# GNN layer on one core: GpSimd gathers every row, transfers carry two node blocks, store rounds lose their empty steps

## The chip, the cores and the metric

One core of a Trainium2 chip runs one program. The time is device microseconds from launch to end, as the runs measure it; a profiled execution gives the trace. The core has TensorE (PE, matmuls; its weight loads are PEld), VectorE (DVE), ScalarE (ACT), GpSimd (POOL) and SyncE (SP). POOL and SP issue most of the transfers here, each in its own fixed order. Sixteen DMA engines move the data.

## The reference

One message-passing layer with a residual and a normalization: 50,000 nodes of 160 features, 1,650,000 edges sorted by destination, four attributes an edge. The last 50,000 edges in the list before sorting are loops from each node to itself.

```python
ss, vv = (s[src], v[src])            # s, v: 64 scalars and 32 vectors of a node
e0 = sh[:, 0:1]; e1 = sh[:, 1:4]     # edge attributes
dot = jnp.einsum('eui,ei->eu', vv, e1)
out0 = C0 * (ss * e0 @ W1 + dot * INV3 @ W2)
...
m = jnp.concatenate([out0, out1.reshape(-1, 3 * MUL1)], axis=1)
m_agg = jax.ops.segment_sum(m, dst, num_segments=n)
...
return x + jax.nn.relu(h)            # h: m_agg times Ws and Wv
...
x = _layernorm(x + _L0_gnn_ref(...))
```

The message is linear in the source row for each attribute. So the kernel may first sum the source rows over a node's edges, weighted by each of the four attributes, and apply the weights after that.

## The kernel before

**Units and pairs.** A unit is 128 edges. Its source rows are gathered into one slot of a tile `xg`, 128 partitions by 160 numbers (`gather`, L314), by one indirect DMA on POOL (L319), whose offsets are a column of `si`. Six units make a group, and two groups a pair: 12 units, one `xg` tile; the pool `rows` holds four such tiles. There are 1,044 pairs; the loop over them (L800) writes out the program, and its order of lines is roughly that of the work.

**What a pair does.** DVE builds a one-hot matrix of the destinations within a window of 32 (`hot`, L328), then multiplies it by the four attributes (`ha`, L331), one pair ahead of its use. PE multiplies `ha` by the gathered rows, unit after unit, and adds up in `ps` (`group_sums`, L343). DVE turns the result into `sums` (L349). Every second pair fills a chunk of four groups; PE applies the combined weights (`phc`, L579) and ACT copies the result out (`hp`, L581). The engines other than SP run in an order that a scheduler makes when the program is built; SP's is as written (L799).

**Node blocks.** Rows of the output come in 391 blocks of 128 nodes. For a block, `ahead` (L588) loads its rows of x and its nodes' own attributes `sa`, seven pairs before the chunks that it needs are complete; `own` (L609) does the loop edge's part (`yx`, L623, then L627 and L629) three pairs before; `block` (L633) adds the chunks with another one-hot matmul (`phb`, L639); then come the normalization (`norm1` to `norm3`, the last being L197 and L199) and `do_send` (L733), which stores the block, eight pairs after the chunk's end. All of these transfers stand on SP's queue.

**Packs.** The loop edges have to be taken out of the list. Except for the first 100 groups, edges go through sixteen packs (`pack`, L408), each up to 128 rows of 790 edges: a pack reads its rows, marks and counts the loop edges, moves the other edges together by copies under a mask in steps of 1, 2, 4, 8 and 16 (L504 to L511, first for the own attributes `pra`, then for the edges `prow`), and stores each row with its own attributes into DRAM (`edges`, `selves`) at a place that SP reads from a table (`store`, L539; `put`, L561). Seventeen store rounds of up to 16 stores each make up a pack. `load` (L247) then reads the packed edges in segments of 20 groups, ten pairs, and `place` (L278) turns them into `si`, destinations and attributes.

**How a pack's steps are dealt.** A pack is a list of steps, some of them empty (`None`). The loop deals the list evenly over the pairs from the pack before to this pack's due time (L834 to L842).

**The helper.** `HELP` (L70) names engines that fetch rows beside POOL. SP has a period of 72 units: for one unit in 72 it reads 128 offsets, 32 at a time, from `ro` (`fetch`, L665; `ro` is made by ACT at L274) and issues 128 plain DMAs of one row each into `xr` (L676), over four pairs. `gather` then leaves that unit out, and `group_sums` uses `xr` as the last rows of its pair.

Behind the loop stands a general path (from L858) that runs only if one of the checks made on the way found data outside the bounds; the run's data are within them.

Of the kernel before, what the change touches and what calls it, by code (L numbers as in the profile page):

```python
# [38 lines left out]
F32 = mybir.dt.float32  # L39
# [6 lines left out]
ET = mybir.EngineType  # L46
# [3 lines left out]
P = 128  # L50
MUL0, MUL1 = 64, 32
D = MUL0 + 3 * MUL1
NK = 4
# [13 lines left out]
PG = 2  # L67
SG = 20

HELP = {ET.SP: 72}  # L70
HEAD = 100
RP = 128
RS = 16
KM = 31
# [29 lines left out]
def tile_gnn_resnorm(ctx: ExitStack, tc: tile.TileContext, x, src, dst, attr, W1, W2, W3, W4, W5, Ws, Wv, out, n_edges):  # L104
    nc = tc.nc
    N = x.shape[0]
    NBLK, NB, GA, G, NU, NG, L, NH, NR, FAR = plan(N, n_edges)
# [83 lines left out]
    def norm2(pool, mv, n):  # L191
        rstd = pool.tile([P, 1], F32, name="rstd")
        nc.scalar.activation(rstd[:n], mv[:n, 1:2], AF.Sqrt, bias=eps_t[:n])  # L193
        return rstd

    def norm3(pool, y, mv, rstd, n):
        nc.vector.reciprocal(rstd[:n], rstd[:n])  # L197
        o = pool.tile([P, D], F32, name="o")
        nc.vector.tensor_scalar(o[:n], y[:n], mv[:n, 0:1], rstd[:n], op0=ALU.subtract, op1=ALU.mult)  # L199
        return o  # L200

# [14 lines left out]
    nblocks = math.ceil(N / P)  # L216
# [8 lines left out]
    with tc.tile_pool(name="once", bufs=1) as once, tc.tile_pool(name="raw", bufs=2) as rawp, \  # L225
# [1 line left out]
            tc.tile_pool(name="far", bufs=3) as farp, \  # L227
            tc.tile_pool(name="ops", bufs=3) as op, tc.tile_pool(name="sums", bufs=4) as sump, \
            tc.tile_pool(name="hp", bufs=alive + 4) as hpp, tc.tile_pool(name="node", bufs=3) as np_, \
            tc.tile_pool(name="ahead", bufs=7) as aheadp, \  # L230
            tc.tile_pool(name="psC", bufs=1, space=PSUM) as psC, tc.tile_pool(name="psK", bufs=2, space=PSUM) as psK, \
            tc.tile_pool(name="psP", bufs=1, space=PSUM) as psP, tc.tile_pool(name="psA", bufs=2, space=PSUM) as psA, \
            tc.tile_pool(name="psM", bufs=2, space=PSUM) as psM, ExitStack() as later_pools:
# [8 lines left out]
        dq = nc.sync  # L242
# [22 lines left out]
        def cast(loaded):  # L265
            s, n, ri, sf, df, af = loaded
            if ri is not None:
                rf = rawp.tile([P, 2, P], F32, name="rf")
                begun.append(nc.scalar.copy(rf[:n], ri[:n]))
                sf, df = rf[:n, 0, :], rf[:n, 1, :]  # L270
            if HELP:

# [85 lines left out]
        def row_start(r):  # L358

            lo, hi = (math.floor(r * L * (1 - 1 / degree)) - 2 * FAR - 2, math.ceil(r * L * (1 - 1 / degree)) + 2 * FAR + 2)  # L360
            return (max(lo, 0), hi if r else 0), (max(math.floor((EH + r * L) / degree) - FAR - 2, 0),
                                                  math.ceil((EH + r * L) / degree) + FAR + 2)

        edges = dram.tile([1, (row_start(NR - 1)[0][1] + L) * C], F32, name="edges")
        selves = dram.tile([1, (row_start(NR - 1)[1][1] + W) * NK], F32, name="selves")
        edge_bytes = edges.bitcast(U8).rearrange("o f -> (o f)")
        self_bytes = selves.bitcast(U8).rearrange("o f -> (o f)")
        rows_stored = [0]
# [39 lines left out]
        def pack(c):  # L408

            r0 = c * RP  # L410
            n = min(RP, NR - r0)
            e0 = EH + r0 * L
            e = slice(e0, e0 + n * L)
            steps, T = [], {}
# [154 lines left out]


            for head, j in [(False, j) for j in range(RS)] + [(True, 0)]:
                steps += [partial(store, head, j), None, None, None]
            return steps + [stored]

        def apply_weights(at, ng):
# [8 lines left out]
        def rows_of(b):  # L584
            nb = min(P, N - b * P)
            return nb, slice(b * P, b * P + nb)

        def ahead(b):  # L588

            nb, row = rows_of(b)  # L590
            xt = aheadp.tile([P, D], F32, name="xt")
            dq.dma_start(xt[:nb], x[row, :])

            assert rows_stored[0] == NR or row_start(rows_stored[0])[1][0] >= row.stop
            sa = aheadp.tile([P, NK], F32, name="sa")
            dq.dma_start(sa[:nb], selves[0, row.start * NK:row.stop * NK].rearrange("(n k) -> n k", k=NK))
            return xt, sa

        def nodes(b):

# [32 lines left out]
        def block(b, xt, t, hot2):  # L633
# [3 lines left out]
            for i, c in enumerate(cs):  # L637
# [7 lines left out]
        pairs = [(s, g, min(PG, NG - g, (s + 1) * SG - g)) for s in range(NSC)  # L645
                 for g in range(s * SG, min(NG, (s + 1) * SG), PG)]
        batches, helped = {}, {}
        for h, (eng, period) in enumerate(HELP.items()):
            first = PG * G + h * period // 2
            nbatch = P // ROWS[eng]  # L650
            while True:
                at = [int(first + i * period / nbatch) // (PG * G) for i in range(nbatch)]
                q = at[-1] + 2
                if q >= len(pairs) or pairs[q][2] < PG:
                    break
                s, g, ng = pairs[q]
                u = (g - s * SG + ng) * G - 1 - len(helped.get(q, []))
                helped.setdefault(q, []).insert(0, (eng, h))
                for i, p in enumerate(at):
                    batches.setdefault(p, []).append((eng, h, q, s, u, i))  # L660
                first += period
# [49 lines left out]
        hps, of_nodes, resid, rstds, outs = {}, {}, {}, {}, {}  # L711
# [4 lines left out]
                of_nodes[b] += (nodes(b),)  # L716

        def do_ahead(b):
            of_nodes[b] = ahead(b)

        def do_own(b):
            of_nodes[b] = own(b, *of_nodes.pop(b))
# [5 lines left out]
            rstds[b] = norm2(np_, resid[b][1], rows_of(b)[0])  # L728

        def do_store(b):  # L730
            outs[b] = norm3(np_, *resid.pop(b), rstds.pop(b), rows_of(b)[0])

        def do_send(b):  # L733
            nb, row = rows_of(b)
            dq.dma_start(out[row, :], outs.pop(b)[:nb])

        def do_cast(s):
            raws[s] = cast(raws[s])
# [179 lines left out]
    with tc.tile_pool(name="edges2", bufs=2) as ep, tc.tile_pool(name="ops2", bufs=2) as op, \  # L918
            tc.tile_pool(name="node2", bufs=1) as np_, tc.tile_pool(name="psA2", bufs=2, space=PSUM) as psA, \
            tc.tile_pool(name="psF2", bufs=1, space=PSUM) as psF:  # L920
        with tc.For_i(0, blocks, 1) as b:
            u0 = table(0, b)
            u1 = table(1, b)
            acc = np_.tile([NBLK, NK, D], F32, name="acc")
            nc.vector.memset(acc, 0.0)

            with tc.For_i(u0, u1, GA) as u:
                u = nc.s_assert_within(u, 0, NU - GA, skip_runtime_bounds_check_because="below u1")
                s_t = ep.tile([P, GA], I32, name="s_t")
                d_t = ep.tile([P, GA], I32, name="d_t")  # L930
                a_t = ep.tile([P, GA, NK], F32, name="a_t")
                e = ds(u * P, GA * P)
                nc.sync.dma_start(s_t, src1[e].rearrange("(p j) o -> p (j o)", j=GA))
                nc.sync.dma_start(d_t, dst1[e].rearrange("(p j) o -> p (j o)", j=GA))
                nc.sync.dma_start(a_t, attr[e].rearrange("(p j) k -> p j k", j=GA))
                rel = ep.tile([P, GA], F32, name="rel2")
                nc.vector.tensor_scalar(rel, d_t, base[:, ds(b, 1)], None, op0=ALU.subtract)
                xg = op.tile([P, GA, D], F32, name="xg2")
                for j in range(GA):
                    nc.gpsimd.indirect_dma_start(  # L940
                        out=xg[:, j, :], out_offset=None, in_=x,
                        in_offset=bass.IndirectOffsetOnAxis(ap=s_t[:, j:j + 1], axis=0))
                hot = op.tile([P, GA, NBLK], F32, name="hotb")
                nc.vector.tensor_tensor(hot, slots[:, :NBLK].unsqueeze(1).to_broadcast([P, GA, NBLK]),
                                        rel.unsqueeze(2).to_broadcast([P, GA, NBLK]), op=ALU.is_equal)
                xa = op.tile([P, GA, NK, D], F32, name="xa")
                nc.vector.tensor_mul(xa, xg.unsqueeze(2).to_broadcast([P, GA, NK, D]),
                                     a_t.unsqueeze(3).to_broadcast([P, GA, NK, D]))
                ps = psA.tile([NBLK, 2, 512], F32, name="ps2")
                for j in range(GA):  # L950
                    for h in range(2):
                        nc.tensor.matmul(ps[:, h, 0:2 * D], hot[:, j, :], xa[:, j, 2 * h:2 * h + 2, :],
                                         start=j == 0, stop=j == GA - 1)
                nc.vector.tensor_add(acc.rearrange("n (h k) f -> n h (k f)", h=2),
                                     acc.rearrange("n (h k) f -> n h (k f)", h=2), ps[:, :, 0:2 * D])
            parts = []
            for h in range(2):
                pt = psF.tile([D // 2, NK, P], F32, name="pt2")
                for k in range(NK):
                    nc.tensor.transpose(pt[:, k, :NBLK], acc[:, k, h * (D // 2):(h + 1) * (D // 2)], ident[:NBLK, :NBLK])  # L960
                at = np_.tile([D // 2, NK, NBLK], F32, name=f"ac{h}")
                nc.scalar.copy(at, pt[:, :, :NBLK])
                parts.append(at)
            ph = psF.tile([NBLK, D], F32, name="ph2")
            i = 0
            for h, at in enumerate(parts):
                for k in range(NK):
                    nc.tensor.matmul(ph, at[:, k, :], BWh[:, h, k, :], start=i == 0, stop=i == 2 * NK - 1)
                    i += 1
            row = ds(b * NBLK, NBLK)  # L970
            xt = np_.tile([NBLK, D], F32, name="xt2")
            nc.scalar.dma_start(xt, x[row, :])
            y, mv = norm1(np_, ph, xt, NBLK)
            o = norm3(np_, y, mv, norm2(np_, mv, NBLK), NBLK)
            nc.scalar.dma_start(out[row, :], o[:NBLK])


# [31 lines left out]
```

## Time and profile before

| | us |
|---|---|
| three runs: median (lowest, highest) | 15674.4 (15671.5, 15689.9) |
| the profiled execution | 15673.7 |
| its span, from the first to the last instruction | 15671.9 |

| engine | busy us | what it mainly does |
|---|---|---|
| POOL | 11694.9 | 12,349 gathers (L319) |
| PE | 8017.6 | 24,698 matmul passes of L343, two for each unit |
| DVE | 6239.3 | `ha` 1802, masked copies of the packs 748, `hot` 555, `sums` 536 |
| ACT | 536.9 | copies out of PSUM |

| DMA issues | count | KB each |
|---|---|---|
| `xr` on SP | 22,144 | 0.6 |
| `edges` from `prow`, on SP | 1,994 and 125 short ones | 18.5 and 0.8 |
| `selves` from `mine`, on SP | 1,992 and 125 short ones | 0.5 and 0.2 |
| x rows, own attributes, output, on SP | 391 each | 80, 2, 80 |
| segments of `edges`, on SP | 100 | 360 |

A line of a group in the profile names the source line, the engine, the operation, and output and input tiles by the program's names; then the number of instructions, their busy time in all and the mean of one in ns, and behind the second bar the engine's idle time just before them with what ended most of it. A line of the timeline has start, duration, engine, line, operation, tiles and, in brackets, the idle time before it and what ended that. A line of the waits has who waited for whom, the sum in us, the number of times and the longest. "issue" stands where the profile shows nothing that the engine waited for. The granted clock of TensorE was 0.737 on average; DMA moved 77 GB/s over the span, with the DMA engines busy about 0.31 of the time.

### The profile page before, as it was taken

The page shows a single profiled execution, that of the slowest core. Times are in us where ns is not written, and L with a number is a line of the kernel's source. Part 1 is how long each engine was busy: PE and PEld are TensorE (multiplying, and loading weights), DVE is VectorE, ACT ScalarE, POOL GpSimd, SP SyncE. Part 2 cuts the span into 40 slices and gives each one's busy share as a digit, 9 for nine tenths or more (in the row PEclk, how much of TensorE's full clock was granted, in tenths as well). Part 3 has the DMA queues.
Part 4 walks back from the last instruction along what each step waited for, and adds up shares of the span by engine and source line. Part 5 has one row for each costly group of instructions (what it writes and reads, how often), then busy time and mean ns, then how long its engine had stood idle before and what let it go on. Part 6 is the DMA issues. An engine that isn't in the chain of part 4 may idle for free. (4 is left out here: it accounts for less than half of the span.)

```text
span 15671.9 us, 167279 instructions
## 1 busy us (share of the span) xinstructions
PE 8017.6 (51%) x38505; PEld 7282.8 (46%) x38506; DVE 6239.3 (40%) x11070; ACT 536.9 (3%) x1497; POOL 11694.9 (75%) x12363
## 2 busy tenths in 40 slices
PE   4555544554555455554555544555555454555555
PEld 3444444444444444444444444444444444444444
DVE  5342525225253442524425243352433525234322
ACT  0000000000000000000000000000000000000000
POOL 7777777777777777777777777777777777777776
PEclk7777777777777777777777777777777777777777
DMA  3323233332333323333233332323333233332322
GB/s 80 86 73 83 71 80 77 77 84 73 78 80 78 82 74 79 80 77 83 72 79 79 78 82 74 83 73 77 82 76 83 74 80 78 78 80 72 77 73 65
DMA packets 843237, 1218.89 MB, mean 78 GB/s; under 512 B 300227, under 2 KB 623912, under 8 KB 838262
## 3 DMA queue, kind: packets, MB, share of 16 engines
q0 software_dynamic: 592752, 1012.42, 26.3%
q1 hardware_dynamic: 248058, 194.45, 4.4%
q8 instruction: 323, 5.29, 0.1%
q14 instruction: 664, 5.44, 0.1%
q10 hardware_dynamic: 1440, 1.29, 0.0%
HBM read 1135.77 MB, written 71.40 MB: 77 GB/s over the span
## 5 line engine op out<-in xcount | busy, mean ns | idle before, releaser
L319 POOL DMA_INDIRECT xg<-in_x,si x12349 | 11690.7, 947 | 3931.0 <-issue 3711.2
L343 PE MATMUL ps<-xg,ha 128*128 128x160 f32 x24698 | 5320.9, 393 | 6189.6 <-DMA xg<-in_x,si 5282.4
L343 PEld LDWEIGHTS ps<-xg,ha 128*128 128x128 f32 x24698 | 5085.6, 268 | 6411.6 <-issue 5473.8
L349 DVE STREAM_TRANSPOSE sums<-ps 128x320 f32<-128x320 f32 x1044 | 535.8, 513 | 6026.3 <-PE ps L343 5912.1
L331 DVE TENSOR_TENSOR ha<-hot,pk 128x1536 f32<-128x1536 f32 x1044 | 1802.3, 1727 | 733.6 <-PE ps L343 721.8
L579 PE MATMUL phc<-BWk,sums 128*128 128x160 f32 x5220 | 919.7, 329 | 784.0 <-DVE sums L349 677.7
L579 PEld LDWEIGHTS phc<-BWk,sums 128*128 128x128 f32 x5220 | 822.6, 210 | 859.5 <-DVE sums L349 720.6
L623 PE MATMUL yx<-BWh,xT 80*128 80x320 f32 x3128 | 1010.1, 469 | 175.3 <-ACT xT L617 175.1
L627 DVE TENSOR_SCALAR t<-yx,sa 128x160 f32<-128x160 f32 x391 | 149.7, 383 | 1830.5 <-PE yx L623 1816.7
L623 PEld LDWEIGHTS yx<-BWh,xT 80*128 80x128 f32 x3128 | 599.9, 202 | 472.7 <-ACT xT L617 264.3
L639 PE MATMUL phb<-hp,hot 128*128 128x160 f32 x3474 | 607.6, 324 | 301.4 <-DVE t L629 300.6
L639 PEld LDWEIGHTS phb<-hp,hot 128*128 128x128 f32 x3474 | 539.7, 207 | 397.8 <-issue 391.0
L328 DVE TENSOR_TENSOR hot<-bank,rel 128x384 f32<-128x384 f32 x1044 | 555.1, 546 | 4.0
L629 DVE SCALAR_TENSOR_TENSOR t<-yx,sa,t 128x160 f32<-128x160 f32 x1173 | 448.5, 382 | 134.9 <-PE yx L623 110.1
L617 ACT COPY xT<-ptx 80x256 f32<-80x256 f32 x391 | 143.5, 367 | 10397.8 <-PE ptx L615 10218.3
L511 DVE COPY_PREDICATED prow<-marks,prow 128x2370 f32<-128x2370 int32 (+8 forms) x160 | 443.4, 2771 | 0.6
L511 DVE COPY_PREDICATED pra<-marks,pra 128x1580 f32<-128x1580 int32 (+8 forms) x160 | 304.9, 1905 | 0.0
L605 DVE TENSOR_TENSOR hot<-bank,rr 128x512 f32<-128x512 f32 (+2 forms) x391 | 288.4, 738 | 0.0
L640 DVE TENSOR_TENSOR phb<-phb,t 128x160 f32<-128x160 f32 x391 | 129.8, 332 | 365.4 <-PE phb L639 361.6
L581 ACT COPY hp<-phc 128x160 f32<-128x160 f32 x522 | 149.8, 287 | 2895.3 <-PE phc L579 2864.4
L193 ACT ACTIVATE rstd<-mv,eps_t 128x1 f32<-128x1 f32 x391 | 115.2, 295 | 1739.4 <-DVE mv L188 1694.6
L615 PE MATMUL ptx<-ident,xt 128*80 128x128 f32 (+1 forms) x782 | 159.2, 287 | 0.0
(148 smaller groups left out, 2856.8 us busy)
## 6 DMA issues: line engine op xcount, KB each, us to landing
xr<-in_x SPq DMA_DIRECT2D x22144, 0.6 KB
xg<-in_x,si POOLq DMA_INDIRECT x12349
edges<-prow SPq DMA_DIRECT2D x1994, 18.5 KB
r<-edges SPq DMA_DIRECT2D x99, 360.0 KB
selves<-mine SPq DMA_DIRECT2D x1992, 0.5 KB
xt<-in_x SPq DMA_DIRECT2D x390, 80.0 KB
out<-o SPq DMA_DIRECT2D x390, 80.0 KB
pra<-in_attr SPq DMA_DIRECT2D x15, 1580.0 KB
```

What stands on the lines that cost most here:

```text
L319: got.append(nc.gpsimd.indirect_dma_start(out=xg[:, j, :], out_offset=None, in_=x, in_offset=bass.IndirectOffsetOnAxis(ap=placed[0][:, u + ...
L328: nc.vector.tensor_tensor(hot[:, :n], slotsP[:, 0:W].unsqueeze(1).to_broadcast([P, n, W]), rel[:, u:u + n].unsqueeze(2).to_broadcast([P, n ...
L331: nc.vector.tensor_tensor(ha[:, :n], hot[:, :n].unsqueeze(2).to_broadcast([P, n, NK, W]), pk[:, :, u:u + n].rearrange("p k u -> p u k").un ...
L343: mm = nc.tensor.matmul(ps[:, j // G, :], ha[:, j].rearrange("p k w -> p (k w)"), xr, start=j % G == 0, stop=j % G == G - 1)
L349: nc.vector.transpose(at[:, :, i:i + ng, :].rearrange("p b g w -> p g b w"), ps[:, :ng].rearrange("p g (b f) -> p g b f", f=FB))
L511: nc.vector.copy_predicated(what[:n, a:e], mi[:, r].unsqueeze(2).to_broadcast([n, e - a, what.shape[2]]), what[:n, a + d:e + d])
L579: nc.tensor.matmul(ph[:ng * W], at[:, b, :ng].rearrange("p g w -> p (g w)"), BWk[:, b, :], start=b == 0, stop=b == ND - 1)
L605: nc.vector.tensor_tensor(hot2[:, :len(cs)], slotsP.unsqueeze(1).to_broadcast([P, len(cs), P]), rr[:, :len(cs)].unsqueeze(2).to_broadcast( ...
L615: nc.tensor.transpose(pt[:, i, :nb], xt[:nb, i * H:(i + 1) * H], ident[:nb, :nb])
L623: nc.tensor.matmul(y[:nb], xT[:, i, :nb], BWh[:, i, ks, :], start=i == 0, stop=i == 1)
L629: nc.vector.scalar_tensor_tensor(t[:nb], y[:nb, i], sa[:nb, k:k + 1], t[:nb], op0=ALU.mult, op1=ALU.add)
L639: nc.tensor.matmul(ph[:nb], hot2[:r, i, :nb], hp[:r], start=i == 0, stop=i == len(cs) - 1)
```

## The change

`HELP` becomes empty: SP fetches no rows singly, `ro` isn't made, and POOL gathers every unit. `ahead`, the output tile and `do_send` work on two neighbouring full blocks at once (`together`; the last block, 80 rows, stands alone): one load of x, one of own attributes, one store, at the first block's time for the loads and at the second's for the store. `norm3` writes into half of the double output tile. The pool `ahead` goes from seven buffers to five, of double tiles for `xt` and `sa`; outputs get a pool of three double tiles. In a pack's list the three empty steps behind each store round are gone, so the list has 77 steps for 128, and the dealing (unchanged) spreads these. One more condition of the planning of helpers changes, which an empty `HELP` never reaches.

```diff
--- before.py
+++ after.py
@@ -67,8 +67,9 @@
 PG = 2
 SG = 20
 
-HELP = {ET.SP: 72}
+HELP = {}
 HEAD = 100
+BP = 2
 RP = 128
 RS = 16
 KM = 31
@@ -193,9 +194,8 @@
         nc.scalar.activation(rstd[:n], mv[:n, 1:2], AF.Sqrt, bias=eps_t[:n])
         return rstd
 
-    def norm3(pool, y, mv, rstd, n):
+    def norm3(o, y, mv, rstd, n):
         nc.vector.reciprocal(rstd[:n], rstd[:n])
-        o = pool.tile([P, D], F32, name="o")
         nc.vector.tensor_scalar(o[:n], y[:n], mv[:n, 0:1], rstd[:n], op0=ALU.subtract, op1=ALU.mult)
         return o
 
@@ -227,7 +227,7 @@
             tc.tile_pool(name="far", bufs=3) as farp, \
             tc.tile_pool(name="ops", bufs=3) as op, tc.tile_pool(name="sums", bufs=4) as sump, \
             tc.tile_pool(name="hp", bufs=alive + 4) as hpp, tc.tile_pool(name="node", bufs=3) as np_, \
-            tc.tile_pool(name="ahead", bufs=7) as aheadp, \
+            tc.tile_pool(name="ahead", bufs=5) as aheadp, tc.tile_pool(name="outs", bufs=3) as outp, \
             tc.tile_pool(name="psC", bufs=1, space=PSUM) as psC, tc.tile_pool(name="psK", bufs=2, space=PSUM) as psK, \
             tc.tile_pool(name="psP", bufs=1, space=PSUM) as psP, tc.tile_pool(name="psA", bufs=2, space=PSUM) as psA, \
             tc.tile_pool(name="psM", bufs=2, space=PSUM) as psM, ExitStack() as later_pools:
@@ -569,7 +569,7 @@
 
 
             for head, j in [(False, j) for j in range(RS)] + [(True, 0)]:
-                steps += [partial(store, head, j), None, None, None]
+                steps.append(partial(store, head, j))
             return steps + [stored]
 
         def apply_weights(at, ng):
@@ -585,16 +585,23 @@
             nb = min(P, N - b * P)
             return nb, slice(b * P, b * P + nb)
 
-        def ahead(b):
-
-            nb, row = rows_of(b)
-            xt = aheadp.tile([P, D], F32, name="xt")
-            dq.dma_start(xt[:nb], x[row, :])
-
-            assert rows_stored[0] == NR or row_start(rows_stored[0])[1][0] >= row.stop
-            sa = aheadp.tile([P, NK], F32, name="sa")
-            dq.dma_start(sa[:nb], selves[0, row.start * NK:row.stop * NK].rearrange("(n k) -> n k", k=NK))
-            return xt, sa
+        def together(b):
+
+            bs = list(range(b // BP * BP, min(nblocks, b // BP * BP + BP)))
+            return bs if all(rows_of(i)[0] == P for i in bs) else [b]
+
+        def ahead(bs):
+
+            nb = rows_of(bs[0])[0]
+            n0, n1 = rows_of(bs[0])[1].start, rows_of(bs[-1])[1].stop
+            xt = aheadp.tile([P, BP, D], F32, name="xt")
+            dq.dma_start(xt[:nb, :len(bs)], x[n0:n1, :].rearrange("(h n) d -> n h d", h=len(bs)))
+
+            assert rows_stored[0] == NR or row_start(rows_stored[0])[1][0] >= n1
+            sa = aheadp.tile([P, BP, NK], F32, name="sa")
+            dq.dma_start(sa[:nb, :len(bs)],
+                         selves[0, n0 * NK:n1 * NK].rearrange("(h n k) -> n h k", h=len(bs), k=NK))
+            return [(xt[:, h], sa[:, h]) for h in range(len(bs))]
 
         def nodes(b):
 
@@ -651,7 +658,7 @@
             while True:
                 at = [int(first + i * period / nbatch) // (PG * G) for i in range(nbatch)]
                 q = at[-1] + 2
-                if q >= len(pairs) or pairs[q][2] < PG:
+                if q >= len(pairs) - 10:
                     break
                 s, g, ng = pairs[q]
                 u = (g - s * SG + ng) * G - 1 - len(helped.get(q, []))
@@ -716,7 +723,9 @@
                 of_nodes[b] += (nodes(b),)
 
         def do_ahead(b):
-            of_nodes[b] = ahead(b)
+            bs = together(b)
+            if b == bs[0]:
+                of_nodes.update(zip(bs, ahead(bs)))
 
         def do_own(b):
             of_nodes[b] = own(b, *of_nodes.pop(b))
@@ -728,11 +737,17 @@
             rstds[b] = norm2(np_, resid[b][1], rows_of(b)[0])
 
         def do_store(b):
-            outs[b] = norm3(np_, *resid.pop(b), rstds.pop(b), rows_of(b)[0])
+            bs = together(b)
+            if b == bs[0]:
+                outs[b] = outp.tile([P, BP, D], F32, name="o")
+            norm3(outs[bs[0]][:, b - bs[0]], *resid.pop(b), rstds.pop(b), rows_of(b)[0])
 
         def do_send(b):
-            nb, row = rows_of(b)
-            dq.dma_start(out[row, :], outs.pop(b)[:nb])
+            bs = together(b)
+            if b == bs[-1]:
+                n0, n1 = rows_of(bs[0])[1].start, rows_of(b)[1].stop
+                dq.dma_start(out[n0:n1, :].rearrange("(h n) d -> n h d", h=len(bs)),
+                             outs.pop(bs[0])[:rows_of(b)[0], :len(bs)])
 
         def do_cast(s):
             raws[s] = cast(raws[s])
@@ -971,7 +986,8 @@
             xt = np_.tile([NBLK, D], F32, name="xt2")
             nc.scalar.dma_start(xt, x[row, :])
             y, mv = norm1(np_, ph, xt, NBLK)
-            o = norm3(np_, y, mv, norm2(np_, mv, NBLK), NBLK)
+            o = np_.tile([P, D], F32, name="o")
+            norm3(o, y, mv, norm2(np_, mv, NBLK), NBLK)
             nc.scalar.dma_start(out[row, :], o[:NBLK])
 
 
```

## The prediction

> **What bounds the kernel now.** I read the busy shares first, then the costliest groups, who waited for whom, and the timeline of GpSimd (POOL) with VectorE (DVE). The chain of waits is no help on this page: each of its shares is 0%.
>
> ```profile
> PE 8017.6 (51%) x38505; PEld 7282.8 (46%) x38506; DVE 6239.3 (40%) x11070; ACT 536.9 (3%) x1497; POOL 11694.9 (75%) x12363
> L319 POOL DMA_INDIRECT xg<-in_x,si x12349 | 11690.7, 947 | 3931.0 <-issue 3711.2
> L343 PE MATMUL ps<-xg,ha 128*128 128x160 f32 x24698 | 5320.9, 393 | 6189.6 <-DMA xg<-in_x,si 5282.4
> POOL xg L319 <- issue: 3711.2, 12175, 0.6
> POOL xg L319 <- PE ps L343: 165.5, 25, 23.2
> ```
>
> POOL shows 75%, but its idle time is 0.30 us after each gather with no releaser: start to start the gathers are 1.25 us apart, and TensorE waits for them (5,282 us). Of the 12,348 distances between starts in the trace, 12,307 lie under 1.4 us, with mean 1.25035 us. The other 41 hold 177.1 us more than that: 13.5 in the first 130 us, 157.0 in fifteen long stalls of 3.4 to 22.9, and 6.6 in small ones. The whole span is then POOL's: first gather at 9.27 + 12,348 x 1.25035 (15,439.3) + 177.1 + the last gather's own 0.95 = 15,626.6, and 45.3 us of tail make 15,671.9. So the change is priced in four terms: number of gathers, distance, stalls, tail.
>
> The longest stall, in the timelines of POOL and of DVE:
>
> ```profile
> 9443.50 0.95 POOL L319 DMA_INDIRECT xg<-in_x,si  x1 [0.30 <-issue]
> 9444.75 0.95 POOL L319 DMA_INDIRECT xg<-in_x,si  x1 [0.30 <-issue]
> 9468.86 0.94 POOL L319 DMA_INDIRECT xg<-in_x,si  x1 [23.16 <-PE ps L343]
> ...
> 9366.68 1.74 DVE L331 TENSOR_TENSOR ha<-hot,pk 128x1536 f32<-128x1536 f32 x1
> 9389.70 5.60 DVE L528 TENSOR_REDUCE mine<-pra 128x128 f32<-128x3200 f32 x1
> 9397.61 2.85 DVE L511 COPY_PREDICATED prow<-marks,prow 128x2370 f32<-128x2370 int32 x1
> 9446.69 0.51 DVE L349 STREAM_TRANSPOSE sums<-ps 128x320 f32<-128x320 f32 x1
> 9460.34 1.75 DVE L331 TENSOR_TENSOR ha<-hot,pk 128x1536 f32<-128x1536 f32 x1
> ```
>
> DVE builds `ha` (L331) once a pair of groups, and TensorE can't multiply a pair without it. Here almost 94 us pass between two of them, filled by the pack's moves (L504 to L528). There are four `xg` buffers of 12 gathers, 15.0 us each: POOL runs ahead until it needs the buffer of a pair that is not multiplied yet, then stands still.
>
> **The change, part by part.**
>
> *Gathers.* SyncE (SP) no longer fetches 22,144 single rows, which are 173 gathers of 128. The order of POOL's instructions in the changed kernel has 12,522 gathers. 173 x 1.25035 = +216.3 us, on the bounding engine, with nothing beside it. SP loses 22,144 issues of 0.32 us (32 took 10.36 us at 75.7 us), some 7.1 ms, and ACT 100 copies of about 0.43 us; neither engine sets the end, so both count zero.
>
> *Distance.* Does a silent SP make a gather shorter? Grouped by the number of `xr` issues that fall in a distance, those with none have mean 1,250.15 ns and those with seven 1,250.13. Grouped by packets of SP's queue: none 1,250.0 ns, four to nine 1,250.4. The gain is bounded by 0.4 ns x 12,522 = 5 us; I take 0, the issue rows being nearest. The Trainium skill, "DMA: Bandwidth & Descriptors", section "Issuing engines are not separate DMA queues", holds that issuing on several engines saves only issue time, "which is usually small relative to the DMA itself". By it the helper is worth next to nothing and the sum would lack the 216; the rows say that issue time is the bound here.
>
> *Store rounds.* A pack had 128 steps dealt over the pairs up to its due time (mostly 60 pairs): 5 to read and begin, 50 of computing, 4 empty, 68 for 17 store rounds (three of four empty), 1 to close. Now the 51 empty ones between stores are gone: 77 steps. The 50 computing steps thus spread over 39 pairs (50/77 of 60) in place of 23 (50/128), and the 17 rounds shrink from 32 pairs to 13. For the effect on `ha` I took DVE's instructions in the order of each kernel, priced each at the mean of its row in this trace, summed what stands between one L331 and the next, and kept a running excess over 15.0 us a pair that never falls below zero. Before: sixteen peaks of 44.5 to 66.7 us, one per pack; every one but the first pack's is followed, four pairs on, by one of the fifteen stalls, and peaks up to 21.4 are followed by none. After: the largest is 15.0 (pair 7, the row table, the same before), all others under 12. Four buffers cover that three times over, so the stalls go: -157.0. Bounds: 0, if the order matters less than I think, and -157.0. I take the latter, since 15 is well on the quiet side of 21.4. The Trainium skill, "SBUF — State Buffer", section "SBUF: two separate sides", speaks against laying more DVE work beside gathers: a vector instruction in a two-port mode locks GpSimd out, which then can't write descriptors. By it the sum would grow with every overlapped instruction. The rows: 2,497 distances fully under DVE work average 1,250.23 ns, 5,988 with none 1,250.28; only beside the row table's 1x2048 instructions were twelve gathers stretched (one to 3.62 us), 13.5 us in all with one 1.83 us IOTA, and those stay.
>
> Each round is 16 stores, 6.3 us of SP; 17/13 rounds a pair make 8.2 us of each 15.0. Before, two rounds ran back to back at 374.7 us (32 stores in 14.2 us), and POOL's gaps there stayed at 0.30 to 0.32. Behind the rounds on SP wait the loads of edges (L254), needed by `place` four pairs, 60 us, later; that cover hides them. If it were gone, a load that came x us late would cost x.
>
> *Two blocks per transfer.* 390 transfers each of x, own attributes and output become 195, SP's 0.4 us each, hidden. Buffers: a double `xt` lives from 7 pairs before to 4 after a block, and 2.7 longer for its partner (391 blocks in 1,044 pairs), some 14 pairs; a new one comes every 5.3, so 2.6 of 5 are in use. Output: 4.7 pairs, about one of 3. A send waits on SP for the second block's norm; behind it are loads with 60 us of cover. DVE's instructions keep their 128x160 shape. All zero.
>
> *Tail.* In the order before, much of the last blocks' work stands behind the last gathered matmul:
>
> ```profile
> 15625.62 0.95 POOL L319 DMA_INDIRECT xg<-in_x,si  x1 [0.30 <-issue]
> 15630.13 0.54 PE L343 MATMUL ps<-xg,ha 128*128 128x160 f32 x2 [1.04 <-DMA xg<-in_x,si]
> 15648.18 0.51 DVE L349 STREAM_TRANSPOSE sums<-ps 128x320 f32<-128x320 f32 x1
> 15654.33 1.52 PE L579 MATMUL phc<-BWk,sums 128*96 128x160 f32 x10
> 15659.99 0.36 DVE L199 TENSOR_SCALAR o<-y,mv,rstd 80x160 f32<-80x160 f32 x1
> ```
>
> After, only one phb matmul, the last phc five and seven phb stand there (one more `xr` product used to close the last pair but one). From the last gather's end: 3.56 to the matmul, 0.58 to the transpose, 0.57 to phc (as 15,648.18 to 15,648.75 before), and from phc's start to the end 17.6 (15,654.33 to 15,671.9): 22.3 in place of 45.3, -23.0. Bounds: 0, and -27 (landing 3.56, transpose and its hand-over 1.15, phc 1.52 and the 11.9 from the last L199 to the end, with nothing between: 18.1).
>
> **Sum**, against the profiled execution's span: 15,671.9 + 216.3 - 157.0 - 23.0 = 15,708.2, that is +36.3 or 0.23%. That execution took 15,673.7 us, 0.7 under the median of the runs; on the median 15,674.4 it makes 15,710.7, say 15,711.
>
> **The rivals.**
>
> *The stalls remain, or others replace them.* For it: the first pack peaks at 58.2 without a stall, so the excess is no perfect gauge; matmuls stand in a new order, and store rounds are denser. Against it: fifteen of sixteen match. With all stalls left 15,711 + 157 = 15,868; with a quarter 15,750.
>
> *A silent SP shortens the distance* (the side that is not slower). About one distance in eight is 1,245 or 1,246 ns long. If all were 1,246, 12,521 x 4.35 ns = 54 us less gives 15,657, 0.1% faster. From 2.9 ns on (36.3/12,521) the change is not slower. Against it: the grouping above, where nothing of SP's moves the mean by more than 0.4 ns.
>
> *The same mechanism, a little cheaper.* If the row table's stretching also falls away (13.5), as its place among the gathers shifts, 15,697 follows.
>
> **How the numbers follow.** What a measurement here tells from no change is about 0.2%, 31 us: 15,706 up. Forecast case (15,700 to 15,725) 0.70, of which 0.19 lies under 15,706; stalls remain in part or new waits arise 0.15 (most of it under 15,750); cheaper by the row table or the tail 0.08; shorter distance 0.05; a different relief that makes it faster 0.02. Slower 0.51 + 0.15 = 0.66; faster 0.02 and 0.01 for the far end of the distance case, 0.03; within 0.2% the rest, 0.19 + 0.08 + 0.04 = 0.31. The range: down to 15,695 for start and tail at their low ends, up to 15,750 for a quarter of the stalls; 0.83 or so lies in it.
>
> **What would show it.** Right: 12,522 gathers; distances still 1.250 us; POOL's wait for `ps` L343 near zero; no gap above 3 us after the first 130 us; the last gather's end near 15,686 and a tail near 22. Wrong: the distance moves by over a nanosecond; a wait of POOL for `ps`, `si` or a landing comes back once per pack; SP's loads of edges reach `place` late; the tail stays at 45.

## The result and the profile after

The changed kernel takes 15,705.09 us (median of 19 runs, 15,703.3 to 15,707.96). The kernel before, run beside it, takes 15,674.9 (19 runs, 15,670.31 to 15,689.89). The ratio is 1.0019, with a 95% interval of 1.0012 to 1.0026: about 30 us slower. The forecast was 15,711. One thing is needed to read the experiments: the first two of the four comparisons ran on other chips, on which the kernel before takes 22,039 and 22,340 us; from those only ratios can be used.

The page of the changed kernel, its span and its costliest groups:

```profile
span 15702.1 us, 120546 instructions
...
PE 8274.5 (53%) x38505; PEld 7583.2 (48%) x38506; DVE 6000.0 (38%) x11070; ACT 498.2 (3%) x1392; POOL 11859.1 (76%) x12536
...
L319 POOL DMA_INDIRECT xg<-in_x,si x12522 | 11854.8, 947 | 3824.4 <-issue 3784.1
```

Its view of who waited for whom, POOL alone (who, for what, us in all, times, longest):

```profile
POOL xg L319 <- issue: 3784.1, 12416, 2.1
POOL xg L319 <- DMA xg<-in_x,si: 17.0, 50, 1.3
...
POOL xg L319 <- PE ps L343: 0.6, 2, 0.3
```

POOL still sets the time: 12,522 gathers, each with its 0.30 us of idle time behind it. Its wait for the product `ps`, 165.5 us before and up to 23.2 at once, is down to 0.6 us. In the starts of the gathers no distance exceeds the usual one by more than 3 us after the first 130 us; before, fifteen did, with 157.0 us in all.

The end of the span, in the timeline:

```profile
15683.15 0.95 POOL L319 DMA_INDIRECT xg<-in_x,si  x1 [0.30 <-issue]
15687.77 0.54 PE L343 MATMUL ps<-xg,ha 128*128 128x160 f32 x2 [1.26 <-DMA xg<-in_x,si]
15688.34 0.35 DVE L349 STREAM_TRANSPOSE sums<-ps 128x160 f32<-128x160 f32 x1 [3.42 <-PE ps L343]
15688.75 1.60 PE L579 MATMUL phc<-BWk,sums 128*96 128x160 f32 x10 [0.17 <-DVE sums L349]
15694.49 0.36 DVE L199 TENSOR_SCALAR o<-y,mv,rstd 80x160 f32<-80x160 f32 x1
```

From the last gather's end (15,684.1) to the end of the span are 18.0 us, where 45.3 were. From the start of the last product to that of its transpose are 0.57 us, where 18.05 were.

The four terms of the prediction, span against span (15,671.9 to 15,702.1):

| term | predicted us | measured us | how measured |
|---|---|---|---|
| 173 gathers more | +216.3 | +216.3 | 12,522 against 12,349, at 1.2502 |
| distance of normal gathers | 0 | -2.2 | 1,250.17 ns against 1,250.35, 12,348 times |
| long stalls | -157.0 | -157.0 | none left |
| tail | -23.0 | -27.3 | 18.0 against 45.3 |
| start and small stretches | 0 | +0.4 | first gather +0.3, first 130 us -0.7, later small ones +0.8 |
| sum | +36.3 | +30.2 | |

### The profile page after: what moved, and what is told of

It reads as the page before. It is cut to its first block, busy times and chain, and to the rows that moved or that the text cites. A ratio compares the mean times of both kernels' runs of the same rounds, so it can differ in the third digit from the quotient of the medians.

```text
span 15702.1 us, 120546 instructions
## 1 busy us (share of the span) xinstructions
PE 8274.5 (53%) x38505; PEld 7583.2 (48%) x38506; DVE 6000.0 (38%) x11070; ACT 498.2 (3%) x1392; POOL 11859.1 (76%) x12536
## 5 line engine op out<-in xcount | busy, mean ns | idle before, releaser
L319 POOL DMA_INDIRECT xg<-in_x,si x12522 | 11854.8, 947 | 3824.4 <-issue 3784.1
L343 PE MATMUL ps<-xg,ha 128*128 128x160 f32 x25044 | 5770.9, 411 | 7141.4 <-DMA xg<-in_x,si 5348.5
L343 PEld LDWEIGHTS ps<-xg,ha 128*128 128x128 f32 x25044 | 5512.6, 283 | 7455.4 <-issue 6701.9
L331 DVE TENSOR_TENSOR ha<-hot,pk 128x1536 f32<-128x1536 f32 x1044 | 1805.9, 1731 | 64.4 <-PE ps L343 64.4
L630 PE MATMUL yx<-BWh,xT 80*128 80x320 f32 x3128 | 1099.9, 498 | 125.3 <-ACT xT L624 123.0
L579 PE MATMUL phc<-BWk,sums 128*128 128x160 f32 x5220 | 852.6, 312 | 11.6 <-DVE t L636 10.2
L630 PEld LDWEIGHTS yx<-BWh,xT 80*128 80x128 f32 x3128 | 642.1, 216 | 423.7 <-ACT xT L624 195.4
L579 PEld LDWEIGHTS phc<-BWk,sums 128*128 128x128 f32 x5220 | 788.7, 201 | 23.8 <-issue 20.1
L646 PE MATMUL phb<-hp,hot 128*128 128x160 f32 x3474 | 550.7, 303 | 0.8 <-ACT hp L581 0.8
L646 PEld LDWEIGHTS phb<-hp,hot 128*128 128x128 f32 x3474 | 499.7, 192 | 24.7 <-issue 23.1
L511 DVE COPY_PREDICATED prow<-marks,prow 128x2370 f32<-128x2370 int32 (+8 forms) x160 | 443.0, 2769 | 0.0
L511 DVE COPY_PREDICATED pra<-marks,pra 128x1580 f32<-128x1580 int32 (+8 forms) x160 | 303.6, 1898 | 0.0
L194 ACT ACTIVATE rstd<-mv,eps_t 128x1 f32<-128x1 f32 x391 | 115.2, 295 | 1334.1 <-DVE mv L189 1329.6
```

The costliest lines, as they stand in the source:

```text
L319: got.append(nc.gpsimd.indirect_dma_start(out=xg[:, j, :], out_offset=None, in_=x, in_offset=bass.IndirectOffsetOnAxis(ap=placed[0][:, u + ...
L331: nc.vector.tensor_tensor(ha[:, :n], hot[:, :n].unsqueeze(2).to_broadcast([P, n, NK, W]), pk[:, :, u:u + n].rearrange("p k u -> p u k").un ...
L343: mm = nc.tensor.matmul(ps[:, j // G, :], ha[:, j].rearrange("p k w -> p (k w)"), xr, start=j % G == 0, stop=j % G == G - 1)
L511: nc.vector.copy_predicated(what[:n, a:e], mi[:, r].unsqueeze(2).to_broadcast([n, e - a, what.shape[2]]), what[:n, a + d:e + d])
L579: nc.tensor.matmul(ph[:ng * W], at[:, b, :ng].rearrange("p g w -> p (g w)"), BWk[:, b, :], start=b == 0, stop=b == ND - 1)
L630: nc.tensor.matmul(y[:nb], xT[:, i, :nb], BWh[:, i, ks, :], start=i == 0, stop=i == 1)
```

## The experiments

The sum came out. But the stalls, its second largest term, were laid to the dealing of the store rounds, and that was an argument: the change also takes the helper away and pairs the transfers, and each could have moved DVE's instructions. So there are two theories. **Dealing**: without the empty steps the pack's work is spread over more pairs, hence DVE has no crowded stretch. **Helper**: DVE's order in the built program is chosen by a scheduler, and it comes out crowded when SP's helper is there and clear when it is not; the dealing is worth nothing.

The gauge of the prediction, the running excess of DVE's work over 15.0 us a pair, was worked out once more for programs that differ in one thing, from each program's own order and the same durations of the kernel before:

| program | peak in each pack, us |
|---|---|
| before | 44.5 to 66.7 |
| before, empty steps out | 58.2 to 86.0 |
| before, helper out | at most 21.1 |
| before, DVE in the order written | at most 11.5 |
| changed | at most 15.0 |
| changed, empty steps put back | at most 17.4 |
| changed, helper put back | 57.6 to 84.3 |

By this gauge the helper theory holds. Beside the helper the dealing even crowds DVE (86.0 for 66.7); without it the dealing loosens DVE a little (at most 15.0 for 17.4), where nothing stalls anyway. The runs test it.

### One part at a time, on the slower chips

The edits, against the kernel before for e1, e2 and e4, against the changed kernel for e3 and f5; f1, f2 and f4 repeat e1, e2 and e4 in the second comparison:

```diff
 e1, f1
-HELP = {ET.SP: 72}
+HELP = {}
 e2, f2
-                steps += [partial(store, head, j), None, None, None]
+                steps.append(partial(store, head, j))
 e3
-HELP = {}
+HELP = {ET.SP: 72}
 e4, f4
-        later_pools.enter_context(tc.manual_schedule(engines={ET.SP}))
+        later_pools.enter_context(tc.manual_schedule(engines={ET.SP, ET.DVE}))
 f5
-HELP = {}
+HELP = {ET.SP: 72}
-                steps.append(partial(store, head, j))
+                steps += [partial(store, head, j), None]
-        later_pools.enter_context(tc.manual_schedule(engines={ET.SP}))
+        later_pools.enter_context(tc.manual_schedule(engines={ET.SP, ET.DVE}))
```

The edit of e4 says that DVE runs its instructions in the order in which the program writes them. No other line changes, but the scheduler still orders the engines that are left to it, and it orders them anew: in the traces TensorE's and ACT's instructions stand in another order than before, too. With the helper in the changed kernel (e3, f5) the altered condition of its planning comes into play, and POOL makes 12,350 gathers, not 12,349.

> The kernel before with an empty HELP and nothing else: single blocks, empty steps between the store rounds. Theory A (as the prediction worked it out): the stalls go because the empty steps go; so here they stay, and the time is 15,675 + 216 = 15,870 to 15,890 us. Theory B: what stands between two L331 on DVE depends on whether the helper is there, since the scheduler that orders DVE and TensorE reckons with SP's queue; the running sum over DVE's order of this kernel peaks at 21 us at most, so no stall over 3 us after the first 130 us, 12,522 gathers, 15,700 to 15,712 us.

> The kernel before with the empty steps between the store rounds taken out and nothing else: helper on, single blocks. Theory A: stalls gone, 12,349 gathers: 15,675 - 157 = 15,518 us. Theory B: the running sum over DVE's order still peaks at 58 to 86 us once per pack (mean 68, before 58), so the fifteen stalls stay or grow by up to 10 us each: 15,675 to 15,850 us.

> The changed kernel with the helper of before put back: double blocks, no empty steps. Theory A: 12,349 gathers and no stalls, 15,705 - 216 = 15,489 us. Theory B: the running sum peaks at 57 to 84 us once per pack, stalls return: 15,650 to 15,830 us.

> The kernel before, with DVE's order too taken as written in place of the scheduler's: helper, single blocks and empty steps as before. The running sum peaks at 11.5 us. Theory B says that the stalls come from DVE's order alone: they go, gathers stay 12,349 at 1.250 us: 15,500 to 15,530 us, 1% faster than before. Rival C: the stalls come from the helper itself (rows that reach TensorE late, or SP's queue), whatever DVE's order: fifteen stalls stay, 15,660 to 15,690 us.

> The same kernel as in the first series (empty HELP alone), where the kernel before took 22,039 us on the chip given, and not 15,675; numbers here are for a chip on which it takes 15,675. Theory A (the dealing of store rounds removes the stalls): stalls stay, 15,870 to 15,890 us. Theory B (the helper's absence changes DVE's order): no stall over 3 us after the first 130 us, 15,700 to 15,712 us.

> Only the empty steps between store rounds taken out; helper and single blocks stay. Theory A: 15,518 us. Theory B: running sum over DVE's order peaks at 58 to 86 us, stalls stay or grow by up to 10 us each, 15,675 to 15,850 us.

> The kernel before with DVE's order as written; helper, single blocks and empty steps as before. Theory B: stalls gone with the helper on, 12,349 gathers: 15,500 to 15,530 us. Rival C (the helper's rows or SP's queue make the stalls): 15,660 to 15,690 us.

> The changed kernel with the helper put back, one empty step behind each store round, and DVE's order as written: double blocks. If stalls follow DVE's order alone, 12,349 gathers without a stall: 15,490 to 15,530 us, 1% faster than both kernels. If double blocks or denser store rounds beside the helper keep SP late (10.4 us of row fetches and 6.3 us of stores can fall in one pair of 15.0), POOL waits for TensorE on the pairs with a helper's unit, some 10 us once per pack: 15,600 to 15,700 us.

| run | us | ratio to before, 95% interval |
|---|---|---|
| e1, helper out | 19,479.32 | 0.8834 (0.8819 to 0.8849) |
| e2, empty steps out | 22,205.87 | 1.0076 (1.0059 to 1.0092) |
| e3, changed with helper | 22,199.91 | 1.0068 (1.0051 to 1.0085) |
| e4, DVE as written | 21,066.17 | 0.9557 (0.9541 to 0.9573) |
| f1, helper out | 19,603.93 | 0.8774 (0.8758 to 0.8789) |
| f2, empty steps out | 22,449.29 | 1.0053 (1.0036 to 1.0069) |
| f4, DVE as written | 21,487.94 | 0.9618 (0.9601 to 0.9635) |
| f5, changed, helper, DVE as written | 21,238.87 | 0.9516 (0.9497 to 0.9535) |

Every expectation in microseconds was worked out for a chip like the first and missed, since the kernel before took 40% longer here. The signs go with the helper theory. Taking the empty steps out alone brought nothing, twice: it cost 0.5 to 0.8%. The changed kernel with the helper put back has the dealing and the pairs, and is 0.7% slower than before. DVE in the order written brought 4%, and nearly 5% in f5 with the pairs and one empty step. Taking the helper out alone brought 12%, far more than the stalls of the first chip could explain, so these runs hold another effect. They can't size the terms, and a gain of 157 us, 0.7% here, could be hidden in it. Where it shows, in the view of waits of e1 (all engines) and of e4 (POOL):

```profile
DVE sums L349 <- remote: 6124.4, 425, 44.1
ACT hp L581 <- remote: 5744.5, 240, 50.6
...
POOL xg L319 <- PE ps L343: 2291.0, 126, 41.6
```

```profile
POOL xg L319 <- PE ps L343: 3823.9, 246, 48.4
```

A gather of e1 takes 949 ns here, against 947 on the first chip, so POOL's own pace is unchanged; but DVE and ACT wait thousands of microseconds for a releaser that the profile doesn't place in the core ("remote"; the traces of before, changed, g2 and h1 have no such wait), and POOL stalls for `ps` even without a helper. What makes these chips so is open, and no size is taken from them.

### The helper alone against the whole change

The third comparison had a chip like the first: the kernel before took 15,678.39 us. g1 is the changed kernel unaltered. g2 has the edit of e1: the kernel before, helper out, empty steps and single transfers kept.

> The changed kernel itself, unaltered, beside the kernel before on the chip that the other experiments get. Where the kernel before takes 15,675 us: 15,705, ratio 1.002. Where the kernel before takes some 22,000 us as in the earlier comparisons: if taking the helper away is what moves the time and the paired transfers and the dealing of the stores are worth nothing, the ratio is that of the helper's removal alone, 0.877 to 0.883 (within 0.01); if the dealing or the pairs count there, it lies more than 0.01 away from it.

> The kernel before with HELP = {} alone: the empties between the store rounds and the single-block transfers stay; 12,522 gathers. Where the kernel before takes 15,675 us: if the dealing of the stores removed the stalls (what the prediction wrote), they stay here and the time is 15,865 to 15,890; if the helper's absence removed them, 15,705 to 15,735 and POOL's wait for ps near zero. Where the kernel before takes some 22,000 us: by the dealing, slower than the changed kernel of the same comparison by 1% or more; by the helper, within 0.5% of it.

g1 took 15,705.41 us (15,703.97 to 15,707.31), ratio 1.0018 (1.0008 to 1.0028). g2 took 15,706.47 us (15,705.13 to 15,708.57), ratio 1.0019 (1.0009 to 1.0028). POOL's waits in g2, and its group:

```profile
POOL xg L319 <- issue: 3778.3, 12403, 0.3
...
POOL xg L319 <- PE ps L343: 0.9, 3, 0.3
```

```profile
L319 POOL DMA_INDIRECT xg<-in_x,si x12522 | 11856.7, 947 | 3822.2 <-issue 3778.3
```

With all fifty-one empty steps of a pack still there, POOL's wait for `ps` is 0.9 us. In the starts of the gathers one distance is 4.3 us over the usual one (a gather that itself took 5.21 us, with no wait), and the tail is 19.6 us. By the dealing theory this kernel had to take 15,865 us or more; it takes 1.06 us more than the whole change. So it was not the dealing that removed the stalls of the changed kernel, and the pairs and the dealing together are worth about a microsecond, which is within the spread of the runs. The whole change is, in its time, the removal of the helper. Whether the dealing could have removed stalls with the helper kept was not run on such a chip; the gauge (58.2 to 86.0) and the signs of e2 and f2 are against it.

### The order alone, with the helper kept

The fourth comparison had such a chip too (before: 15,679.51 us). h1 has the edit of e4. It keeps the helper, the empty steps and the single transfers.

> The kernel before with its helper, its empties and its single-block transfers, only that DVE's instructions keep the order in which the program writes them (12,349 gathers, as before). Where the kernel before takes 15,675 us: if the stalls come from the order in which DVE's work is put, the fifteen of them (157 us) go and, with the tail of 45 us or one shortened by up to 23, the time is 15,490 to 15,520, ratio 0.988 to 0.990. If the stalls come from the helper's own fetching (single rows that land late, SP's queue), they stay: 15,660 to 15,680. Where the kernel before takes some 22,000 us: ratio 0.955 to 0.963, as twice before.

h1 took 15,492.94 us (15,491.9 to 15,494.16), ratio 0.9882 (0.9866 to 0.9898). Its page, and DVE's `ha` (L331) with the pack's moves in its timeline, in the pack whose stall was the longest before:

```profile
span 15490.4 us, 167602 instructions
...
L319 POOL DMA_INDIRECT xg<-in_x,si x12349 | 11688.9, 947 | 3771.0 <-issue 3732.1
```

```profile
9298.69 1.75 DVE L331 TENSOR_TENSOR ha<-hot,pk 128x1536 f32<-128x1536 f32 x1
...
9309.02 5.50 DVE L528 TENSOR_REDUCE mine<-pra 128x128 f32<-128x3200 f32 x1
...
9316.49 1.75 DVE L331 TENSOR_TENSOR ha<-hot,pk 128x1536 f32<-128x1536 f32 x1
...
9320.97 2.88 DVE L511 COPY_PREDICATED prow<-marks,prow 128x2370 f32<-128x2370 int32 x1
...
9324.32 1.75 DVE L331 TENSOR_TENSOR ha<-hot,pk 128x1536 f32<-128x1536 f32 x1
```

The reduction L528 and a masked copy L511 stand here each between two `ha`, 17.8 and 7.8 us apart, where almost 94 us passed before. The largest distance between two `ha` in the whole run is 49.5 us. There are 12,349 gathers as before, and no long stall.

The distance alone isn't the sign of a stall, however. The changed kernel has up to 72.1 us between two `ha` (from 12,077 us on) and g2 up to 77.4, without a stall, and before there are stalls beside distances of 50.1 and 51.7. What differs is how much work DVE has there: it is busy for 20 of those 72.1 us, and for 72 of the 94 of the longest stall. Nor is it `ha` alone that comes late. TensorE before the longest stall of the kernel before:

```profile
9433.01 3.01 PE L639 MATMUL phb<-hp,hot 128*128 128x160 f32 x10 [36.45 <-DVE t L629]
...
9447.25 3.03 PE L579 MATMUL phc<-BWk,sums 128*128 128x160 f32 x10 [10.71 <-DVE sums L349]
...
9462.14 6.45 PE L343 MATMUL ps<-xg,ha 128*128 128x160 f32 x24 [3.42 <-DVE ha L331]
```

TensorE stands 36.5 us for DVE's `t`, 10.7 for `sums` and 3.4 for `ha`. In the 75 us before the end of each of the fifteen long stalls, its waits of over 1 us for `t` and `sums` add up to between 29.7 and 62.5 us, those for `ha` to at most 3.6. So `t` and `sums`, too, stand behind the pack's moves.

So the stalls were neither the price of the helper's fetching nor of the empty steps: they came from the order that the scheduler made, and with DVE in the order written the helper is a clean gain. One thing is not separated: TensorE's order changes in h1 as well. That DVE's order is what counts is argued from the gauge. It reads DVE alone, and of the kernels with at most one helper on chips like the first it tells the one with stalls (before, 44.5 us or more in each pack) from the three without (changed, g2 and h1, at most 21.1). Against the changed kernel the span of h1 is 211.7 us shorter: the 173 gathers that it spares are 216.3, its tail is 25.6 us in place of 18.0 (-7.6), its distance 0.14 ns longer (-1.7), its start and small stretches 4.8 shorter. h1 beats both kernels.

### Two helpers

If one helper gives 216 us, a second one on ACT should give more. h2 is the changed kernel with these edits:

```diff
-HELP = {}
+HELP = {ET.SP: 72, ET.Activation: 72}
-                steps.append(partial(store, head, j))
+                steps += [partial(store, head, j), None]
-        later_pools.enter_context(tc.manual_schedule(engines={ET.SP}))
+        later_pools.enter_context(tc.manual_schedule(engines={ET.SP, ET.DVE}))
```

> The changed kernel with two helpers, SP and ACT, each fetching one gather's rows in 72, one empty step after each store in place of three, and DVE's order as written: 12,179 gathers. Where the kernel before takes 15,675 us: if gathers are worth 1.250 us each and the stalls stay away by DVE's order, 12,179 x 1.25035 = 15,228 + first gather 9 + start and small ones 20 + tail 20 to 45 = 15,277 to 15,302, ratio 0.975 to 0.976. If helpers bring stalls of their own (a late row, a busier SP or ACT), 15,430 or more. Where the kernel before takes some 22,000 us the helpers cost more than they bring: ratio 0.94 to 1.0.

It took 17,744.46 us (17,737.81 to 17,778.96), ratio 1.1323 (1.1304 to 1.1342). Both bounds of the hopeful case missed by over 2,400 us, and the rival named only a floor. Its view of waits:

```profile
ACT rstd L194 <- DVE mv L189: 12947.3, 340, 162.3
...
PE ps L343 <- DMA xr<-in_x: 4214.2, 141, 121.1
...
POOL xg L319 <- PE ps L343: 2007.9, 79, 83.9
```

The first line is not idle time alone: sending transfers doesn't count as busy, and for some 8,240 of its 12,947 us ACT was sending rows. TensorE waits for single rows (`xr`) that land late, and POOL for TensorE: 68 long stalls, 2,448 us in all. One of them, in the timelines of SP's and ACT's queues, of TensorE and of POOL:

```profile
594.65 45.97 ACTq L683 DMA_DIRECT2D xr<-in_x  x101
646.65 0.29 ACT L194 ACTIVATE rstd<-mv,eps_t 128x1 f32<-128x1 f32 x1 [53.45 <-DVE mv L189]
646.73 71.59 ACTq L683 DMA_DIRECT2D xr<-in_x  x155
```

```profile
589.94 0.28 SPq L563 DMA_DIRECT2D edges<-prow  x1
597.94 0.24 SPq L563 DMA_DIRECT2D selves<-mine  x1
598.38 0.23 SPq L563 DMA_DIRECT2D edges<-prow  x1
601.40 0.23 SPq L563 DMA_DIRECT2D selves<-mine  x1
...
718.34 0.23 SPq L563 DMA_DIRECT2D selves<-mine  x1
718.66 0.23 SPq L563 DMA_DIRECT2D edges<-prow  x1
...
757.90 10.71 SPq L683 DMA_DIRECT2D xr<-in_x  x32
```

```profile
770.02 0.87 PE L343 MATMUL ps<-xr,ha 128*128 128x160 f32 x2 [110.70 <-DMA xr<-in_x]
```

```profile
690.90 0.95 POOL L319 DMA_INDIRECT xg<-in_x,si  x1 [0.30 <-issue]
782.02 0.94 POOL L319 DMA_INDIRECT xg<-in_x,si  x1 [90.17 <-PE phc L579]
```

ACT sends 101 rows up to 640.6 us, waits 6.0 us in an ACTIVATE (L194) for DVE (the other 46 of the 53.45 are the sending), and then sends 155 more in one burst up to 718.3. While a burst runs, SP's stores often leave several microseconds apart; from 718.3 on most leave every 0.32 us. Over the whole run the distance from one store (L563) to the next with no other transfer of SP's between, gaps over 30 us left out, is 547 ns on average (median 323) where ACT has issued nothing in the microsecond before the first of the two, and 2,237 ns (median 1,283) where it has. SP falls behind, its last 32 rows of a batch go out at 757.9 us, and TensorE goes on 1.4 us after the last of them, after 110.7 us of standing. This is a reading of one trace. With SP's helper alone (h1, whose store rounds keep their empty steps) the same distance is 394 ns. One helper with the same dealing was not run on a chip like this one, so how much belongs to ACT's bursts and how much to the denser store rounds stays open.

## Why the prediction was right, and which step of it was not

**Gathers**: right. 12,522 as counted, at 1.250 us each, nothing beside them. h1 shows the price from the other side: the helper kept and the stalls gone, the kernel is 212 us faster than the changed one.

**Stalls**: the amount was right to the decimal (157.0 predicted, none left), and not by luck, since the gauge read the order of the whole built program; the cause was wrong. The step "Store rounds" said that the 51 empty steps are gone, "the 50 computing steps thus spread over 39 pairs in place of 23", and took the clear order of DVE for the result of that. The gauge was worked out on the whole changed program, which differs in three things, and its answer was written down to one of them. g2 undoes the dealing and the pairs and has no stalls to speak of; e2 and f2, on the slower chips, have the dealing and win nothing. The right sentence would have been: DVE's order changes as the helper goes, and with it go the stalls. The chain of the stall was also told too narrowly: `ha` is the last that TensorE waits for, but `t` and `sums` hold it longer (36.5 and 10.7 us against 3.4 in the longest). The step "Gathers" correspondingly counted the helper's removal as a pure cost of 216 us, where by g2 it carries the whole change: +216 for gathers, -157 for stalls, -26 for the tail. A reader who trusted the step would have kept the dealing and put the helper back, and e3 shows that this kernel is no faster than the one before, by its sign at least, on a slower chip.

**Distance**: 0 taken with a bound of -5; measured -2.2. With SP silent a gather is a little shorter: 1,250.17, 1,250.16 and 1,250.16 ns in the three traces without a helper (changed, g1, g2), 1,250.35 and 1,250.31 with it (before, h1). The row grouped by SP's packets had shown up to 0.4 ns, and the issue rows show it too if they are read whole: 4,100 distances that hold four `xr` issues average 1,250.49 ns, 6,028 with none 1,250.27. No such distance holds seven; that row counts with each issue the register move beside it. DVE's work costs a gather as little: the 2,483 distances wholly under it average 1,250.46 ns in the trace of before and the 5,980 with none 1,250.27, where the prediction has 1,250.23 and 1,250.28.

**Two blocks per transfer**: zero, right as far as is shown. g1 against g2 is 1.06 us, for the pairs and the dealing together.

**Tail**: -23.0 predicted, -27.3 measured. The order of the last instructions was read rightly, but the stretch from the last L199 to the end was carried over as 11.9 us and measured 7.6; that is the whole miss of 4.3. It goes with the helper: 7.5 us in g2, 12.1 in h1. The row of before could not price it, since this stretch changes with what the change removes.

**The rivals**: no stalls came back on a chip like the first; the distance fell by 0.18 ns, far from the 2.9 that would decide; the row table's stretching stayed (12.8 us in the first 130 against 13.5).

The Trainium skill, "DMA: Bandwidth & Descriptors", section "Issuing engines are not separate DMA queues", which the prediction weighed, says that a second issuing engine saves only the time of issuing, and that all DMAs interleave on the same engines whoever issues them. The runs agree with the first and show that it needn't be small: the issue time of 173 gathers is worth 216 us in h1, since the gathers' issue is the bound. h2, with a further issuer and denser store rounds, was 13% slower than before; whether interleaving is the reason no run here shows.

## What to carry to other kernels

When a change has several parts and a gauge is taken from the built program, take it once for each part alone before naming the part that moved it; the number can be right while its cause is wrong, and the better kernel hides behind the wrong cause. Where a scheduler chooses an engine's order, a part that seems to touch only another engine can reorder it: if a stall goes away with such a part, fix the order itself and keep the part. Here that is one word in a list, and it is 1.2% faster than before and 1.4% faster than the change.

## What the hardware showed that was not expected

The closing INC_SWDGE_SEM of POOL takes 0.464 us in the three kernels without single-row fetches (changed, g1, g2), 1.235 in the two with one helper (before, h1), and 2.086 with two (h2). The stretch from the start of the last L199 to the end grows beside it: 7.5 to 7.6 us, 12.0 to 12.1, and 16.1. The instruction's own growth is only 0.8 to 0.9 us of each step, and the rest is not explained.

In h2, with two engines issuing small DMAs, the one lost far more than the other: beside ACT's row fetches SP's stores went from 547 to 2,237 ns apart, while ACT's row fetches went from 491 to 637 ns apart beside transfers of SP's (gaps over 30 us left out in both).

The kernel before, 15,675 to 15,680 us in three comparisons at a granted clock of 0.74, took 22,039 and 22,340 us on two other chips at 0.66 and 0.65. The gather itself was the same there (949 ns in e1, 947 in f1).
